# The values of a chunk between the two score rounds of the next one, in a two-layer cross-attention network

## The chip, the cores and the metric

The kernel runs on one core of one Trainium2 chip. The metric is the device time of one execution in microseconds (us); the number quoted is a median over runs. A profile is one further execution, recorded by the hardware profiler, and every duration of a single instruction below comes from it.

## The reference

Two equal layers, each of self-attention, cross-attention to a context, and a gated feed-forward, every one of them after a layer norm and with a residual. All in float32; batch 4, 512 queries, width 320, 20 heads of 16, a context of 1601 rows of width 192.

```
h1 = _ln(x, n1_g, n1_b)
x = _attn(h1, h1, q1, k1, v1, o1_w, o1_b, heads) + x
h2 = _ln(x, n2_g, n2_b)
x = _attn(h2, context, q2, k2, v2, o2_w, o2_b, heads) + x
h3 = _ln(x, n3_g, n3_b)
a, g = jnp.split(h3 @ ff_w1 + ff_b1, 2, axis=-1)
x = a * gelu(g) @ ff_w2 + ff_b2 + x

# _attn, per head
sim = jnp.einsum('bhid,bhjd->bhij', q, k) * scale
out = jnp.einsum('bhij,bhjd->bhid', softmax(sim), v)
```

## The kernel before

**Units and chunks.** Attention is cut into units: one layer, one kind (self or cross), one batch, one group of four heads. Each layer has 20 self units and 20 cross units, so there are 80 in all. The keys of a unit are cut into chunks of 128: four chunks in a self unit (512 keys), thirteen in a cross unit (1601 keys, the last chunk of 65). That makes 160 self chunks and 520 cross chunks, 680 in all. Feed-forward units follow the cross units of each layer.

**A chunk's scores.** For each head of a chunk TensorE (PE) computes a 128x512 tile `st` of scores with keys on the partitions: two products (line 1113, a high and a low part of the queries) and a third matmul that subtracts the row maximum (line 1116). Each uses 32 rows of the array, the rows of its head, so that four such matmuls can run beside each other on four row groups. ScalarE (ACT) then takes the exponential of the tile from PSUM into SBUF (line 1126).

**Two rounds.** A chunk goes in two rounds. The first has the scores of heads 0 and 1, and beside them, on the row groups of heads 2 and 3, two products `sps` (line 926) for the maxima of a coming unit. The second has the scores of heads 2 and 3 and maxima on row groups 0 and 1. VectorE (DVE) reduces the maxima from PSUM (line 947).

**Values.** `values` multiplies the exponentials by the values (line 1141 before, line 1140 after): per chunk four heads, each on 32 columns of the array and 128 rows of keys, all into one PSUM tile `av`. A float32 matmul stands as two matmuls in the trace, so a chunk is eight of them. The result is accumulated in SBUF tile `o`: the first is copied (line 1152), and each later one is copied by ACT to a spare place (line 1157) and added by GpSimd (POOL, line 1158). In the last unit ahead of a feed-forward stage DVE does it instead (line 1154). In cross units `values` takes two chunks at a time, which accumulate in one `av`; in self units one.

**The order on PE.** It is written out by hand, one instruction stream. `main` issues for each chunk the first round, the second round, any extra maxima, then `flush()`, which runs what is in `late`: the values of the chunk (or two chunks) before. Then it appends this chunk's `values` to `late`, and `steps` picks other work off queues (projections of queries, keys and values of coming units, output projections, norms) by due times and credits. Below, this other work on PE is called a step.

**PSUM.** The tiles `st`, `av` and most tiles of the steps come from one pool of four banks, `ps_st`, handed out in turn; so a tile waits until the tile that came four before it has been read. The maxima use a second pool, `ps_m`, of two.

**Places.** Exponentials and the ACT copies of `av` go in turn to thirteen SBUF buffers in cross units and ten in self units (`place`); a buffer is written again when its reader is done.

Of the kernel before, what the change touches and what calls it, by code (L numbers as in the profile page):

```python
# [19 lines left out]
H, DH = 20, 16  # L20
# [3 lines left out]
P = 128  # L24
NQ = N // P
G, HG = 5, 4
GD = HG * DH
SLOT = 32
GT = GD // SLOT

VW = DH + 1
# [33 lines left out]
def kernel(ctx: ExitStack, tc: tile.TileContext, x, context, ws, out):  # L65
# [18 lines left out]
    nc = tc.nc  # L84
# [16 lines left out]
    columns_of = const.tile([P, NC2 * H * VW + SLOT - VW], F32, name="vals")  # L101
# [61 lines left out]
    def place():  # L163
        these = places[at_place["kind"]]
        at_place["i"] = (at_place["i"] + 1) % len(these)
        return these[at_place["i"]]
# [113 lines left out]
    units = []  # L280
# [44 lines left out]
    start = {"on": True, "both": False}  # L325
# [25 lines left out]
    def pick():  # L351
        heads = [
            (q[0][1] + late_by(n), n)
            for n, q in chains.items()
            if q and q[0][2]() and q[0][3]() and (q[0][0][0] != LIGHT or clock["lights"])
        ]
        return min(heads)[1] if heads else None

    def run(chain):
        costs, _, ready, _, f = chains[chain].popleft()  # L360
        assert ready(), chain
        f()
        clock["credit"] -= sum(costs)
# [15 lines left out]
    def next_cost():  # L379
        name = pick()  # L380
        return None if name is None else sum(chains[name][0][0])

    def tick():
        clock["round"] += 1
        clock["credit"] = max(-2.0, min(4.0, clock["credit"] + pace()))

    def steps(beside, lights=1):


        tick()  # L390
        clock["lights"], clock["slots"] = lights, 4
        clock["tiles"] = True if beside is None else None
        done = 0
        while True:
            name = pick()
            if name is None:
                break
            cost = sum(chains[name][0][0])
            if cost >= 0.1:
                share = (2.2, 1.1) if beside else (9.0, 9.0) if beside is False else (0.5, 0.75, 1.5)  # L400
                least = cost * share[done] if done < len(share) else 3.0
                if clock["credit"] < (3.0 if beside is False else least):
                    break
                done += 1
                if clock["tiles"] is not None:
                    clock["tiles"] = name in ALIKE
            run(name)
            if cost == LIGHT:
                clock["lights"] -= 1
            clock["slots"] -= name == "slots"  # L410
        clock["tiles"] = None

    def until(test, name):
        while not test():
            assert chains[name], name
            run(name)
# [570 lines left out]
    def max_reduce(u):  # L987
        if u.pm is not None:
            nc.vector.tensor_reduce(
                u.nm.rearrange("p (j t) -> p t j", t=NQ), u.pm, AX.X, ALU.max, negate=True  # L990
            )
# [89 lines left out]
    late = []  # L1081

    def flush():
        for f in late:
            f()
        late.clear()

    def round_of(scores, maxima):

        todo = [f() for f in scores] + [f() for f in maxima]  # L1090
        for i in range(max((len(passes) for passes, _ in todo), default=0)):
            for passes, _ in todo:
                if i < len(passes):
                    passes[i]()
        for _, then in todo:
            then()

    def main(u, give, nxt):

        pr = {}  # L1100
        if at_place["kind"] != u.kind:
            at_place.update(kind=u.kind, i=min(at_place["i"], len(mine) - 1))

        def score(c, j, st=None):
            r = min(P, u.nkeys - c * P)
            rows = slice(j * SLOT, (j + 1) * SLOT)
            if st is None:
                st = ps_st.tile([P, N], F32, tag="st", name="st")
            keys = u.kT[rows, u.k0 + u.cols[c] : u.k0 + u.cols[c] + r].bitcast(F32R)
            two_rows = slice(j * SLOT, j * SLOT + 2)  # L1110

            def product(e):
                nc.tensor.matmul(st[:r, :], lhsT=keys, rhs=u.q[rows, e, :].bitcast(F32R), start=(e == 0), stop=False)  # L1113

            def less_maximum():
                nc.tensor.matmul(  # L1116
                    st[:r, :],
                    lhsT=units_of[two_rows, :r].bitcast(F32R),
                    rhs=u.mrow[two_rows, :].bitcast(F32R),
                    start=False,  # L1120
                    stop=True,
                )

            def exponential():
                p = place()
                nc.scalar.activation(p[:r], st[:r], AF.Exp)  # L1126
                pr[c, j] = p

            return [lambda: product(0), lambda: product(1), less_maximum], exponential

        last = nxt is None or nxt.kind == "ff"

        def values(cs):
            if u.g in (0, 2):
                until(lambda: units[u.i - u.g].vmade[u.g // 2] > cs[-1], "values")
            ps = ps_st.tile([P, N], F32, tag="st", name="av")
            for c in cs:
                r = min(P, u.nkeys - c * P)
                for j in range(HG):
                    head = (c * H + u.g * HG + j) * VW  # L1140
                    nc.tensor.matmul(  # L1141
                        ps[j * SLOT : (j + 1) * SLOT, :],
                        lhsT=columns_of[:r, head : head + SLOT],
                        rhs=pr.pop((c, j))[:r, :],
                        start=(c == cs[0]),
                        stop=(c == cs[-1]),
                    )
            u.valued = cs[-1] + 1

            if cs[0] == 0:  # L1150
                u.o = three.tile([P, N], F32, tag="o", name="o")
                (nc.vector.tensor_copy if last else nc.scalar.copy)(u.o, ps)
            elif last:
                nc.vector.tensor_tensor(u.o, ps, u.o, ALU.add)
            else:
                vo = place()
                nc.scalar.copy(vo, ps)  # L1157
                nc.gpsimd.tensor_tensor(u.o, u.o, vo, ALU.add)  # L1158
            if u.valued == u.nch:
                add_finish(u)  # L1160


        n = 2 if u.cross else 1
        together = {min(c + n, u.nch) - 1: list(range(c, min(c + n, u.nch))) for c in range(0, u.nch, n)}

        for c in range(u.nch):
            extra = []
            if last:

                both = ps_m.tile([P, 2, N], F32, tag="m", name="st")  # L1170
                round_of([lambda j=j: score(c, j, both[:, j % 2] if j > 1 else None) for j in range(HG)], [])
                tick()
            else:
                for odd in range(2):
                    if odd:
                        tick()
                    pair, rounds = give(2 * c + odd)
                    extra += rounds
                    round_of([lambda j=j: score(c, j) for j in ((2, 3) if odd else (0, 1))], pair)
            u.scored = c + 1  # L1180

            start["both"] = True
            if extra:
                round_of([], extra[0])
            start["both"] = False
            flush()
            if c in together:
                late.append(lambda cs=together[c]: values(cs))
            steps(None, 1 if extra or c == u.nch - 1 else 2)
            for i, e in enumerate(extra[1:]):  # L1190
                if i and next_cost() is not None:
                    run(pick())
                start["both"] = True
                round_of([], e)
                start["both"] = False
            if not last and c == u.nch - 3:
                max_reduce(nxt)
                max_end(nxt)
            if loads:
                loads.popleft()()  # L1200
# [300 lines left out]
```

## Time and profile before

| | |
|---|---|
| runs (us) | 3257.41, 3266.63, 3268.47; median 3266.63 |
| profiled execution (us) | 3267.39; its span, first to last instruction, 3265.6 |
| granted TensorE clock | 0.967 of full speed |
| PE busy | 3117.7 us, 95% of the span |
| DVE busy | 2077.9 us, 64% |
| ACT busy | 1866.6 us, 57% |
| POOL busy | 972.6 us, 30% |
| maxima reduced, line 947 into `pm`, DVE | 980 instructions, mean 1195 ns |
| exponentials, line 1126 into the 8 `pr` buffers, ACT | 1791, mean 602 ns |

Self-attention takes about 30 to 470 us and 1650 to 2050 us of the span, cross-attention about 470 to 1380 us and 2050 to 2990 us, and feed-forward nearly all of the rest. PE counts as busy while any matmul is in its array, and the ends of matmuls are modelled; so a stretch of PE that is "busy" can still hold waits. What a stretch of PE work costs is therefore read from starts: from the first matmul of one kind of work to the first matmul of the next.

### The profile page before, as it was taken

How to read it: one execution, taken by the hardware profiler on the slowest of the kernel's cores; microseconds unless marked ns; L12 is line 12 of the kernel's file. 1: busy time of each engine (PE TensorE's matmuls, PEld its weight loads, DVE VectorE, ACT ScalarE, POOL GpSimd, SP SyncE). 2: the span in 40 equal slices, each digit the busy share in tenths (PEclk: the TensorE clock that was granted, in tenths of full speed). 3: DMA queues.
4: the chain of work that ended last, by engine and by line, in shares of the span. 5: the costliest groups of instructions: out<-in, count | busy, mean ns of one | idle time of the engine just before them, and what ended most of it. 6: DMA issues, size and time to landing. Idle time of an engine off the chain costs nothing.

```text
span 3265.6 us, 89144 instructions
## 1 busy us (share of the span) xinstructions
PE 3117.7 (95%) x36690; PEld 1686.7 (52%) x36690; DVE 2077.9 (64%) x2833; ACT 1866.6 (57%) x3721; POOL 972.6 (30%) x1141
## 2 busy tenths in 40 slices
PE   7899899999999999999998998999999999999999
PEld 3455455555455555455444554555555555554555
DVE  6766777777777776522246777777777777774221
ACT  3666566776667676711126665667767777765110
POOL 2435232323323332111114453324233333322000
PEclk8999899999999999999989998999999999999999
DMA  3433222211212211200113332212112111112000
GB/s 92 91 65 77 44 43 45 54 39 38 65 33 42 60 35 28 80 4 6 27 23 73 72 62 44 41 40 51 33 39 55 36 41 39 39 22 65 9 10 15
DMA packets 213039, 145.08 MB, mean 44 GB/s; under 512 B 65556, under 2 KB 203160, under 8 KB 212632
## 3 DMA queue, kind: packets, MB, share of 16 engines
q1 hardware_dynamic: 211368, 138.32, 19.1%
q8 instruction: 289, 4.73, 0.6%
q10 hardware_dynamic: 1264, 1.06, 0.1%
q14 instruction: 118, 0.97, 0.1%
HBM read 33.04 MB, written 7.93 MB: 13 GB/s over the span
## 4 chain that ended last, share of the span: by engine, by line
PE 80%; DVE 8%; ACT 4%; issue 3%; DMA 2%; SPq 2%; POOL 1%; ACTq 0%; DVEq 0%; POOLq 0%
PE av L1141 19%; PE st L1113 19%; PE fps L1246 9%; PE st L1116 6%; PE yps L1302 5%; PE sps L926 5%; DVE pm L947 3%; PE kps L779 3%; PE qps L717 3%; PE vps L869 3%; PE ops L1050 3%; DVE nmax L947 2%; PE fps L1259 2%; ACT pr L1126 2%; PE kps L749 1%
## 5 line engine op out<-in xcount | busy, mean ns | idle before, releaser
L947 DVE TENSOR_REDUCE pm<-sps 128x2 f32<-128x1024 f32 (+1 forms) x980 | 1127.6, 1195 | 225.3 <-PE sps L926 199.6
L1113 PE MATMUL st<-q,kT 32*128 32x512 f32 (+1 forms) x5440 | 1089.3, 445 | 40.5 <-DVE x L1057 8.0
L1126 ACT ACTIVATE pr<-st 128x512 f32<-128x512 f32 (+1 forms) x1791 | 947.1, 602 | 269.9 <-PE st L1116 252.1
L926 PE MATMUL sps<-kT,q 32*128 32x512 f32 (+1 forms) x6400 | 993.6, 411 | 52.9 <-DMA kT<-stage 20.1
L1113 PEld LDWEIGHTS st<-q,kT 32*128 32x128 f32 (+1 forms) x5440 | 537.6, 182 | 482.3 <-ACT pr L1126 160.2
L1116 PE MATMUL st<-m,units 2*128 2x512 f32 (+1 forms) x2720 | 655.3, 400 | 5.9 <-issue 2.1
L1141 PE MATMUL av<-pr,vals 128*32 128x512 f32 (+1 forms) x3582 | 644.5, 636 | 16.9 <-ACT pr L1126 10.3
L1158 POOL TENSOR_TENSOR o<-o,pr 128x512 f32<-128x512 f32 x236 | 302.2, 1281 | 951.2 <-ACT pr L1157 931.2
L926 PEld LDWEIGHTS sps<-kT,q 32*128 32x128 f32 x6400 | 474.1, 188 | 103.6 <-DVE pm L947 33.3
L947 DVE TENSOR_REDUCE nmax<-sps 128x2 f32<-128x1024 f32 (+1 forms) x356 | 381.2, 1109 | 175.2 <-PE sps L926 121.6
L1126 ACT ACTIVATE wself<-st 128x512 f32<-128x512 f32 (+1 forms) x801 | 427.6, 602 | 75.1 <-PE st L1116 68.6
L1116 PEld LDWEIGHTS st<-m,units 2*128 2x128 f32 (+1 forms) x2720 | 350.7, 184 | 42.8 <-issue 7.7
L1141 PE MATMUL av<-wself,vals 128*32 128x512 f32 (+1 forms) x1602 | 344.5, 635 | 3.6 <-ACT pr L1126 3.0
L1246 PE MATMUL fps<-hT,w 128*128 128x512 f32 x640 | 285.4, 599 | 1.8 <-DVE pr L1272 0.9
L1269 ACT ACTIVATE pr<-fps,b 128x512 f32<-128x512 f32 x80 | 50.6, 683 | 370.4 <-PE fps L1259 268.1
L1141 PEld LDWEIGHTS av<-pr,vals 128*32 128x32 f32 (+1 forms) x3582 | 114.3, 112 | 236.9 <-issue 101.4
L1158 POOL TENSOR_TENSOR o<-o,wself 128x512 f32<-128x512 f32 x89 | 114.0, 1281 | 381.5 <-ACT wself L1157 381.5
L1157 ACT COPY pr<-av 128x512 f32<-128x512 f32 x236 | 140.9, 597 | 135.7 <-PE av L1141 134.7
L1246 PEld LDWEIGHTS fps<-hT,w 128*128 128x128 f32 x640 | 118.9, 190 | 151.8 <-issue 146.6
L624 POOL TENSOR_SCALAR stage<-stage 128x256 fp32r<-128x256 f32 (+1 forms) x155 | 107.1, 691 | 218.6 <-ACT stage L725 135.5
L624 POOL TENSOR_SCALAR w<-w 128x896 fp32r<-128x896 f32 x40 | 98.1, 2452 | 147.0 <-DVE w L789 118.5
L1050 PE MATMUL ops<-wo,aT 112*32 112x160 f32 (+1 forms) x3072 | 128.5, 303 | 4.1 <-ACT pr L1126 2.8
(100 smaller groups left out, 3020.8 us busy)
## 6 DMA issues: line engine op xcount, KB each, us to landing
kT<-w SPq DMA_DIRECT2D x160, 192.0 KB
q<-stage SPq DMA_DIRECT2D x320, 64.0 KB
q<-stage SPq DMA_DIRECT2D x154, 128.0 KB
aT<-o SPq DMA_DIRECT2D x320, 32.0 KB
m<-turned SPq DMA_DIRECT2D x636, 2.0 KB
kT<-stage SPq DMA_DIRECT2D x156, 64.0 KB
w<-in_L_xattn_ff_w_dram SPq DMA_DIRECT2D x20, 256.0 KB
ctxT<-ctxT SPq DMA_DIRECT2D x24, 208.0 KB
```

Of the source, the lines that this page charges most:

```text
L624: eng.tensor_scalar(high.bitcast(F32R), x, 1.0, None, ALU.mult)
L926: nc.tensor.matmul(out, lhsT=u.q[rows, e, queries].bitcast(F32R), rhs=u.kT[rows, keys].bitcast(F32R), start=(e == 0), stop=(e == 1),)
L947: nc.vector.tensor_reduce(to[:, j : j + n], part, AX.X, ALU.max, negate=(ns == 1))
L1050: nc.tensor.matmul(ps[f : f + m, : D // 2], lhsT=aT[:n, k, t * P + f : t * P + f + m], rhs=wo[:n, k, cols], start=(k == 0), stop=(k == 2),)
L1113: nc.tensor.matmul(st[:r, :], lhsT=keys, rhs=u.q[rows, e, :].bitcast(F32R), start=(e == 0), stop=False)
L1116: nc.tensor.matmul(st[:r, :], lhsT=units_of[two_rows, :r].bitcast(F32R), rhs=u.mrow[two_rows, :].bitcast(F32R), start=False, stop=True,)
L1126: nc.scalar.activation(p[:r], st[:r], AF.Exp)
L1141: nc.tensor.matmul(ps[j * SLOT : (j + 1) * SLOT, :], lhsT=columns_of[:r, head : head + SLOT], rhs=pr.pop((c, j))[:r, :], start=(c == cs[0] ...
L1157: nc.scalar.copy(vo, ps)
L1158: nc.gpsimd.tensor_tensor(u.o, u.o, vo, ALU.add)
L1246: nc.tensor.matmul(ps, lhsT=w1[:, k, i * FF + c * P : i * FF + (c + 1) * P], rhs=u.hT[:, k, :], start=ahead and k == 0, stop=not ahead and ...
L1302: nc.tensor.matmul(ps[:, :D], lhsT=hid[c][:, t * P : (t + 1) * P], rhs=w2[:, c, :], start=(c == 0), stop=(c == NHC - 1),)
```

## The change

The body of `values` is the same but for one chunk instead of a list of chunks. In cross units too each chunk now has its own `av` tile and its own evacuation. `flush()` is called once more, between the first and the second round of a chunk, so that the values of the chunk before stand there. The call behind the rounds stays, and finds nothing in `late` except in units whose chunks go in one round (the last unit ahead of a feed-forward stage).

```diff
-        def values(cs):
+        def values(c):
             if u.g in (0, 2):
-                until(lambda: units[u.i - u.g].vmade[u.g // 2] > cs[-1], "values")
+                until(lambda: units[u.i - u.g].vmade[u.g // 2] > c, "values")
             ps = ps_st.tile([P, N], F32, tag="st", name="av")
-            for c in cs:
-                r = min(P, u.nkeys - c * P)
-                for j in range(HG):
...
-                        start=(c == cs[0]),
-                        stop=(c == cs[-1]),
+            r = min(P, u.nkeys - c * P)
+            for j in range(HG):
...
+                    start=True,
+                    stop=True,
...
-        n = 2 if u.cross else 1
-        together = {min(c + n, u.nch) - 1: list(range(c, min(c + n, u.nch))) for c in range(0, u.nch, n)}
-
         for c in range(u.nch):
...
                     round_of([lambda j=j: score(c, j) for j in ((2, 3) if odd else (0, 1))], pair)
+                    if not odd:
+                        flush()
             u.scored = c + 1
...
             flush()
-            if c in together:
-                late.append(lambda cs=together[c]: values(cs))
+            late.append(lambda c=c: values(c))
             steps(None, 1 if extra or c == u.nch - 1 else 2)
```

More of the change, by code (lines that the diff above doesn't have):

```diff
@@ L1131, in main @@
         last = nxt is None or nxt.kind == "ff"
-        def values(cs):
+        def values(c):
             if u.g in (0, 2):
-                until(lambda: units[u.i - u.g].vmade[u.g // 2] > cs[-1], "values")
+                until(lambda: units[u.i - u.g].vmade[u.g // 2] > c, "values")
             ps = ps_st.tile([P, N], F32, tag="st", name="av")
-            for c in cs:
-                r = min(P, u.nkeys - c * P)
-                for j in range(HG):
[L1140 to L1144, printed above, removed]
-                        start=(c == cs[0]),
-                        stop=(c == cs[-1]),
-                    )
-            u.valued = cs[-1] + 1
-            if cs[0] == 0:
+            r = min(P, u.nkeys - c * P)
+            for j in range(HG):
+                head = (c * H + u.g * HG + j) * VW
+                nc.tensor.matmul(
+                    ps[j * SLOT : (j + 1) * SLOT, :],
+                    lhsT=columns_of[:r, head : head + SLOT],
+                    rhs=pr.pop((c, j))[:r, :],
+                    start=True,
+                    stop=True,
+                )
+            u.valued = c + 1
+            if c == 0:
                 u.o = three.tile([P, N], F32, tag="o", name="o")
```

## The prediction

> **What bounds the kernel now.** I read the page first, for the engine that carries the span.
>
> ```profile
> span 3265.6 us, 89144 instructions
> PE 3117.7 (95%) x36690; PEld 1686.7 (52%) x36690; DVE 2077.9 (64%) x2833; ACT 1866.6 (57%) x3721; POOL 972.6 (30%) x1141
> PE 80%; DVE 8%; ACT 4%; issue 3%; DMA 2%; SPq 2%; POOL 1%; ACTq 0%; DVEq 0%; POOLq 0%
> ```
>
> PE is the bound (95% busy, 80% of the chain that ended last); the rest has room. But PE executes in order, and a "busy" PE can still be waiting with a matmul in flight. So I then read the timeline of single chunks, PE and ACT side by side (columns: start, length, engine, line, what). First a cross chunk that stands between two calls of values:
>
> ```profile
> 645.24 0.50 PE L1113 MATMUL st<-q,kT 32*128 32x512 f32 x2
> 645.58 0.40 PE L1113 MATMUL st<-q,kT 32*128 32x512 f32 x2
> 645.81 0.40 PE L1116 MATMUL st<-m,units 2*128 2x512 f32 x1
> 646.07 0.49 PE L1113 MATMUL st<-q,kT 32*128 32x512 f32 x1
> 646.31 1.09 ACT L1126 ACTIVATE pr<-st 128x512 f32<-128x512 f32 x2 [0.29 <-PE st L1116]
> 646.42 0.61 PE L1116 MATMUL st<-m,units 2*128 2x512 f32 x2
> 646.96 1.07 PE L1141 MATMUL av<-pr,vals 65*32 65x512 f32 x8
> 647.96 0.45 PE L779 MATMUL kps<-ctxT,w 32*64 32x224 f32 x8
> ```
>
> Three things are to be seen. Matmuls of 512 columns follow each other by phases: 0.34 us after the first, then 0.23. Two adjacent rounds share a phase, because the second round's heads are on the row groups that the first has left: five phases for a chunk, not six. And the values start at 646.96, which is 0.05 us after the first exponential is over (646.31 + 0.60 = 646.91): their `av` tile takes the bank of `st` of head 0. So a chunk costs 1.72 us from its first score to the values, where five phases with the passage at the end would be 0.33 + 3 x 0.23 + 0.33 = 1.35.
>
> Second, two chunks in a row with nothing between, and the values of two chunks behind:
>
> ```profile
> 908.43 0.50 PE L1113 MATMUL st<-q,kT 32*128 32x512 f32 x2
> 910.14 0.98 PE L1113 MATMUL st<-q,kT 32*128 32x512 f32 x2 [0.26 <-ACT pr L1126]
> 911.20 0.91 PE L1113 MATMUL st<-q,kT 32*128 32x512 f32 x2
> 911.98 0.60 PE L1116 MATMUL st<-m,units 2*128 2x512 f32 x2
> 912.51 0.63 PE L1141 MATMUL av<-wself,vals 128*32 128x512 f32 x3
> ```
>
> From 908.43 to 912.51: 4.08 us for two chunks, where ten phases need 2.50. The second chunk waits for exponentials to give banks back. Third, a block of only three phases, from a chunk without maxima:
>
> ```profile
> 1351.43 0.74 PE L1113 MATMUL st<-q,kT 32*128 32x512 f32 x8
> 1351.99 0.41 PE L1116 MATMUL st<-m,units 2*128 2x512 f32 x4
> 1352.33 1.06 PE L1141 MATMUL av<-pr,vals 65*32 65x512 f32 x8
> ```
>
> It takes 0.90 us. Last, two rows of the costliest groups, for what a call of values leaves to other engines:
>
> ```profile
> L1158 POOL TENSOR_TENSOR o<-o,pr 128x512 f32<-128x512 f32 x236 | 302.2, 1281 | 951.2 <-ACT pr L1157 931.2
> L1157 ACT COPY pr<-av 128x512 f32<-128x512 f32 x236 | 140.9, 597 | 135.7 <-PE av L1141 134.7
> ```
>
> **Off PE.** The cross units now evacuate 13 times instead of 7: 38 units x 6 = 228 more copies of 0.59 us on ACT (135 us, 57% to about 59%) and 228 more adds of 1.28 us on POOL (292 us, 30% to about 37%). In the two last units 12 adds of 0.69 us go to DVE (8 us). I price all this at nothing: POOL stays idle for over half of the time, and an exponential that takes over a place that POOL reads comes thirteen places later, now 2.6 chunks (some 8 us) instead of 2.9. If that cover failed, each late add would hold an exponential, and the values and PE behind it, for up to 1.28 us.
>
> **On PE, block by block.** The order of PE's instructions in both programs gives the blocks, that is stretches of one kind of work. Without extra maxima and without the last units, before has 345 score blocks of one chunk, 97 of two; values of two chunks stand 129 times before scores and 109 times before a step, values of one 57 and 141 times. Medians from first matmul to the next block's first matmul, over the whole trace: 1.71, 4.07; 1.854, 1.741, 0.996, 0.882. The sum is 590 + 395 + 239 + 190 + 57 + 124 = 1595 us. 101 blocks with extra maxima (85 of one chunk, 16 of two) hold 145 + 66 = 211 us of the same; the extra maxima themselves stay.
>
> After, the scores fall apart: 655 blocks of a single round, 266 of two rounds (the second of a chunk and the first of the next, where no step stands between them), 74 and 21 with extra maxima, and 674 calls of values, all with scores behind them. Score blocks go from 565 to 1053 in all.
>
> One round alone: three phases, 0.33 + 0.23 + 0.33 = 0.90. No such block is in the trace with two heads and two maxima. The nearest row is the block of 1351.43, the same three phases, so I take 0.90. It can't be less; it can be no more than the 1.71 of two rounds. Two of them cost 1.80 where the chunk cost 1.71: the phase that adjacent rounds shared is lost and a passage is added, but the wait for the bank (0.37) goes, since `av` now takes a bank whose exponential ran long before.
>
> A two-round block: here a new wait comes. The values behind it are those of the chunk whose second round has only just opened the block. Subtracting the maximum starts 0.57 after the block does, ends 0.40 later, ACT starts 0.10 later, two exponentials take 1.09, and PE starts 0.05 after them: 0.57 + 0.40 + 0.10 + 1.09 + 0.05 = 2.20 us, against 1.35 that PE needs. ACT is free for it: the copy of the `av` before begins about 0.2 into the block and is over by 0.8, the exponentials can start at 1.07. Queued behind the waiting values on PE are the chunk's next second round and any step; ACT waits for that round in turn. The bounds are 1.35 (nothing waits) and 2.79 (the copy gets between, 0.59).
>
> Where a step does stand between the rounds, the shortest (query projections, about 0.8 us) gives 0.90 + 0.8 + 0.90 = 2.6, more than 2.20, so there the values find their exponentials done.
>
> The sum after: 655 x 0.90 + 266 x 2.20 + 674 x 0.996 = 590 + 585 + 671 = 1846; with extra maxima 74 x 0.90 + 21 x 2.20 = 113; the last units 24 x 1.8 = 43, before 12 x 1.9 = 23. Context values on row tiles, like the scores, lose a passage each: 64 x 0.25 = 16 off. So after 1846 + 113 + 43 - 16 = 1986, before 1595 + 211 + 23 = 1829: 157 us more. From this I take 25 us, because in the self stages PE is idle for 84 us (840 us, 756 busy) for other engines, and some of the added time lies in those waits. That leaves +132 us on 3267.4: 3399, call it 3400. The profiled execution is 0.8 us above the median of the runs, so no correction is made.
>
> **A rule that speaks against the change.** In the trace a passage from scores to values starts 0.325 us after the last phase where nothing waits, against a pitch of 0.23, and from values to scores 0.523 against 0.43: 0.19 us for leaving and returning, 488 times more often, 92 us; this is already inside the block times. The Trainium skill, TensorEngine Tiling (Array Packing), section Key Properties, says that a change of tiling mode drains TensorE, but gives no price. The Trainium skill, TensorE: Matmul & The Clock Gate, section Step-by-step: what each phase is for, has about 128 cycles for a drain; an estimate from that page, at its 2.4 GHz, is 53 ns each, 52 us for 976 passages, and the forecast would be some 40 us lower by it; I keep the trace's rows.
>
> **Rivals.** (1) Faster: the values don't wait for the last exponential in a two-round block. Then it costs 1.35, 266 x 0.85 = 226 us less, and the kernel comes to 3400 - 226 = 3174; the place is the `av` matmul behind the second round, and with 2.20 - 132/266 = 1.70 us per block the change would be even. For it: the two-chunk blocks lose 1.57 us each to banks now, and the change breaks these up. Against it: the five terms of 2.20 are each read from rows above and follow one another. (2) Slower by more: one-round blocks wait too, because ACT, with its 228 more copies and the steps' evacuations in its order, is behind at short steps, or POOL holds a place. Half the 1.09 us of two exponentials on half of the blocks is 655 x 0.27 = 180 us: 3580. For it: the exponentials are on the chain at every chunk now. Against: 2.6 us of cover against 2.20. (3) No change: PE's stalls now (block means exceed the medians, and PE is idle for 148 us in all) absorb all that is added: 3267. Against: 520 of the 680 chunks are cross chunks, and in the cross stages (2030 us) PE is idle for only 48 us. That the change does nothing is no rival, since the order of instructions differs.
>
> **How the numbers follow.** A measurement of this kernel can tell about 0.3% (10 us) from no change. The forecast has 0.82; its own range is 3320 to 3470, from a two-round block of 1.90 (80 us less) to one-round blocks of 1.00 (65 us more). Rival 1 and partial forms of it 0.06, rival 2 0.09, rival 3 0.03. The range is 3320 to 3480, with a little of rival 2. Chances: faster 0.06, same 0.03, slower 0.91.
>
> **What would show it.** Right: in the profile after, `av` waits for ACT `pr` or `wself` (line 1126) for many times the 22 us that it has now; blocks of two rounds take 2.2 us and of one round 0.9; adds on POOL go from 348 to 576; PE's share falls to about 92%. Wrong: two-round blocks near 1.4, one-round blocks over 1.1, exponentials that wait for POOL, or maxima that wait for banks.

## The result, and the profile after

The changed kernel takes 3388.81 us (median of 4 runs, 3378.96 to 3391.92), the kernel before 3267.55 (4 runs): ratio 1.0365, 95% interval 1.0324 to 1.0406. It is slower by 121 us; the forecast was 132 us, 3400. The page of the changed kernel, its span, its engines and the shares of the chain that ended last:

```profile
span 3388.5 us, 89789 instructions
PE 3274.0 (97%) x36690; PEld 1625.3 (48%) x36690; DVE 2123.4 (63%) x2846; ACT 2027.4 (60%) x3949; POOL 1264.9 (37%) x1369
PE 84%; DVE 9%; SPq 3%; DMA 2%; issue 1%; ACT 1%; POOL 1%; ACTq 0%; DVEq 0%; POOLq 0%
```

PE has the same 36690 matmuls and is "busy" for 156 us more. Where that is can be read in a timeline of PE and ACT (start, length, engine, line): a two-round block, which begins with the second round of one chunk and ends with the first round of the next, the values behind it, and a one-round block.

```profile
742.57 0.50 PE L1113 MATMUL st<-q,kT 32*128 32x512 f32 x2
742.76 0.59 ACT L1156 COPY wself<-av 128x512 f32<-128x512 f32 x1
743.13 0.40 PE L1116 MATMUL st<-m,units 2*128 2x512 f32 x1
743.62 2.06 ACT L1126 ACTIVATE wself<-st 128x512 f32<-128x512 f32 x4 [0.28 <-PE st L1116]
744.28 0.62 PE L1140 MATMUL av<-pr,vals 128*32 128x512 f32 x2
744.75 1.06 PE L1140 MATMUL av<-wself,vals 128*32 128x512 f32 x3
745.74 0.50 PE L1113 MATMUL st<-q,kT 32*128 32x512 f32 x2
746.30 0.41 PE L1116 MATMUL st<-m,units 2*128 2x512 f32 x2
746.64 0.86 PE L717 MATMUL qps<-hT,w 112*32 112x128 f32 x24
```

ACT starts the exponentials at 743.62; the second is over at 744.71 (0.60 + 0.49 later), and the values of the last head start within the row of 744.75. The values' first three heads began at 744.28, 0.06 us after the first exponential (743.62 + 0.60) had given its bank back. So block and values take 745.74 - 742.57 = 3.17 us; the prediction had 2.20 + 1.00. Over the trace the median of this sum is 3.175 us, in 254 blocks that carry eight maxima matmuls. The one-round block goes from 745.74 to 746.64: 0.90 us, the median 0.90 as well.

Two signs in the profile that the prediction got wrong. PE's share rose to 97% and did not fall to 92%, and the waits of PE say next to nothing of the values:

```profile
PE sps L926 <- DVE pm L947: 26.9, 26, 1.5
PE av L1140 <- ACT pr L1126: 0.8, 3, 0.3
```

The reason is in the timeline: the values' last head waits while the other three are in the array, so PE counts as busy. The wait shows in the length of the values (1.457 us median behind such a block, 0.996 elsewhere), not in an idle time. Nor did the waits of the values' weight loads for exponentials grow: for those in `pr` and `wself` together 177 us before (133.3 and 44.1), 176 after (113.9 and 62.4).

Off PE, the groups of the evacuation are as forecast; the adds on POOL are 576 over all places (348 before), and ACT's exponentials wait less than 1 us for them:

```profile
L1157 POOL TENSOR_TENSOR o<-o,pr 128x512 f32<-128x512 f32 x377 | 483.0, 1281 | 804.7 <-ACT pr L1156 799.0
L1156 ACT COPY pr<-av 128x512 f32<-128x512 f32 x377 | 221.3, 587 | 45.8 <-PE av L1140 42.1
```

### The profile page after: what moved, and what is told of

The parts are those of the page before. It is cut to its first block, busy times and chain, and to the rows that moved or that the text cites. A ratio compares the mean times of both kernels' runs of the same rounds, so it can differ in the third digit from the quotient of the medians.

```text
span 3388.5 us, 89789 instructions
## 1 busy us (share of the span) xinstructions
PE 3274.0 (97%) x36690; PEld 1625.3 (48%) x36690; DVE 2123.4 (63%) x2846; ACT 2027.4 (60%) x3949; POOL 1264.9 (37%) x1369
## 3 DMA queue, kind: packets, MB, share of 16 engines
q14 instruction: 124, 1.02, 0.1%
## 4 chain that ended last, share of the span: by engine, by line
PE 84%; DVE 9%; SPq 3%; DMA 2%; issue 1%; ACT 1%; POOL 1%; ACTq 0%; DVEq 0%; POOLq 0%
PE av L1140 21%; PE st L1113 20%; PE fps L1242 8%; PE st L1116 7%; PE yps L1298 5%; PE sps L926 4%; PE qps L717 3%; DVE pm L947 3%; PE kps L779 3%; PE ops L1050 3%; PE vps L869 2%; PE fps L1255 2%; DVE nmax L947 2%; PE vps L851 2%; PE kps L749 2%; SPq L1006 2%
## 5 line engine op out<-in xcount | busy, mean ns | idle before, releaser
L947 DVE TENSOR_REDUCE pm<-sps 128x2 f32<-128x1024 f32 (+1 forms) x980 | 1150.8, 1196 | 369.4 <-PE sps L926 354.2
L1113 PE MATMUL st<-q,kT 32*128 32x512 f32 (+1 forms) x5440 | 1059.3, 455 | 15.1 <-DVE pm L947 5.4
L926 PE MATMUL sps<-kT,q 32*128 32x512 f32 (+1 forms) x6400 | 1016.1, 419 | 45.5 <-DVE pm L947 26.9
L1113 PEld LDWEIGHTS st<-q,kT 32*128 32x128 f32 (+1 forms) x5440 | 468.0, 186 | 783.0 <-issue 340.8
L1157 POOL TENSOR_TENSOR o<-o,pr 128x512 f32<-128x512 f32 x377 | 483.0, 1281 | 804.7 <-ACT pr L1156 799.0
L1140 PE MATMUL av<-pr,vals 128*32 128x512 f32 (+1 forms) x3582 | 761.3, 628 | 7.6 <-DVE nmax L947 2.6
L1116 PE MATMUL st<-m,units 2*128 2x512 f32 (+1 forms) x2720 | 611.4, 407 | 21.5 <-DMA m<-turned 18.7
L1140 PE MATMUL av<-wself,vals 128*32 128x512 f32 (+1 forms) x1604 | 418.0, 621 | 1.4 <-DVE pm L947 0.7
L1157 POOL TENSOR_TENSOR o<-o,wself 128x512 f32<-128x512 f32 x175 | 224.6, 1284 | 315.6 <-ACT wself L1156 314.8
L1116 PEld LDWEIGHTS st<-m,units 2*128 2x128 f32 (+1 forms) x2720 | 304.2, 187 | 79.1 <-issue 28.3
L1156 ACT COPY pr<-av 128x512 f32<-128x512 f32 x377 | 221.3, 587 | 45.8 <-PE av L1140 42.1
```

The source lines that it names most:

```text
L926: nc.tensor.matmul(out, lhsT=u.q[rows, e, queries].bitcast(F32R), rhs=u.kT[rows, keys].bitcast(F32R), start=(e == 0), stop=(e == 1),)
L947: nc.vector.tensor_reduce(to[:, j : j + n], part, AX.X, ALU.max, negate=(ns == 1))
L1116: nc.tensor.matmul(st[:r, :], lhsT=units_of[two_rows, :r].bitcast(F32R), rhs=u.mrow[two_rows, :].bitcast(F32R), start=False, stop=True,)
L1140: nc.tensor.matmul(ps[j * SLOT : (j + 1) * SLOT, :], lhsT=columns_of[:r, head : head + SLOT], rhs=pr.pop((c, j))[:r, :], start=True, stop= ...
```

## The experiments

The change has two halves: the values go one chunk at a time, and they stand between the rounds. The first four kernels take these apart, and the wait from the rest.

**Single chunks behind both rounds.** The changed kernel without the call in the middle:

```diff
-                    if not odd:
-                        flush()
```

> One half of the change alone: values one chunk at a time, but still behind both score rounds. Theory A (the cost of the change is the wait of the values for the exponentials of the round that stands just ahead, plus a small loss per split chunk): nothing is split here, and the 97 two-chunk score blocks with two chunks of values behind (4.07 + 1.85 us) become two chunks at 1.71 + 1.00 each, so 97 x 0.5 = 48 us less, some 4 us more for passages: about 3224 us, faster than before. Rival B (the cost is passages between kinds of PE work: 121 us for 488 more score blocks, 0.25 us each): 689 score blocks instead of 565, 124 x 0.25 = 31 us more: about 3298 us.

Measured: 3226.97 us, ratio to before 0.9873 (0.985 to 0.9895), granted clock 0.968. The forecast of theory A (3224) holds, that of rival B (3298) does not: there are 124 more score blocks than before and the kernel is 41 us faster. So passages (changes on PE from one kind of work to another) alone do not set the time, and of the two halves this one is a gain; the place between the rounds costs 3389 - 3227 = 162 us. This kernel beats both others. What bounds its chunk is the wait that the prediction read in the profile of before, now at most chunks. PE and ACT in its timeline, and the waits of weight loads (PEld), which show a wait that PE's own rows hide:

```profile
902.79 0.60 ACT L1126 ACTIVATE pr<-st 128x512 f32<-128x512 f32 x1 [0.65 <-PE st L1116]
903.44 1.07 PE L1140 MATMUL av<-pr,vals 128*32 128x512 f32 x8 [0.27 <-ACT pr L1126]
PEld av L1140 <- ACT pr L1126: 197.9, 410, 0.9
```

The values start 0.05 us after the end of the first exponential of the two rounds just ahead (902.79 + 0.60 = 903.39): their `av` tile takes the bank of that score tile.

**Pairs between the rounds.** The kernel before with the call in the middle:

```diff
+                    if not odd:
+                        flush()
```

> The other half alone: values between the two rounds, but two chunks of a cross unit at a time as before. Theory A, by block prices (score blocks of one round 0.90, of three about 2.9, of four 4.07; values of two chunks 1.85): the first chunk of a pair covers most of the wait for the second chunk's exponentials, and the two-chunk stalls of before stay: about 55 us more than before, 3320 us. Rival B: 815 score blocks, 250 x 0.25 = 62 us more, 3329 us. This run does not tell A from B; it tells the place from the cutting into single chunks.

Measured: 3415.95 us, 1.0467 (1.0436 to 1.0498): the slowest of all, 96 us over the expectation. The blocks of four rounds, 45 of them, take 5.12 us on average where I had 4.07 (the 31 that no window of half clock touches 4.78), those of three rounds about 3.15 where I had 2.9, and the granted clock of its runs has the median 0.952. What makes the four rounds longer at full clock was not taken apart. The changed kernel, with single chunks at the same place, is 27 us faster.

**Values one chunk later.** The changed kernel with

```diff
-    def flush():
-        for f in late:
-            f()
-        late.clear()
+    def flush(keep=0):
+        while len(late) > keep:
+            late.pop(0)()
...
-                        flush()
+                        flush(1 if u.cross and c else 0)
...
-            flush()
+            flush(1 if u.cross and not last else 0)
```

> The changed kernel, with the values of a cross unit run one chunk later still (between the rounds of chunk c stand the values of chunk c-2, not c-1; at the first chunk of a unit both that are left). PE's blocks are nearly the same (1015 score blocks, 1053 in the changed kernel). Theory A: the values find their exponentials done; a two-round block with its values goes from 3.18 us to what ACT needs per chunk (four exponentials 2.06, one copy 0.59, gaps 0.1: 2.75 us) or less, so about 205 x 0.43 = 88 us less than the changed kernel: 3300 us, down to 3230 if PE's own 2.35 us were reached. Rival B: no change but for 38 blocks, about 3380 us.

Measured: 3387.19 us, 1.036 (1.0312 to 1.0409), no change against the changed kernel. At the block it did what theory A said: two-round block and values fell from 3.175 to 2.725 us (median of 178). But the time didn't follow. The granted clock of its four runs has the median 0.9475, against 0.9615, some 46 us at 3.3 us per 0.001 (see the end); and since the second chunk of a unit has no values between its rounds now, 37 blocks of three or four rounds came back, at 3.1 to 4.7 us each. In its profile the values take 89 us less than in the changed kernel, scores with maxima 57 us more and the steps 8 us more.

**Cross units only.** The call in the middle stands in cross units alone:

```diff
-                    if not odd:
+                    if not odd and u.cross:
                         flush()
```

> The changed kernel with the new place in cross units only; self units have their values behind both rounds as before. Theory A: in self units the change cost 0.2 us per chunk with a step behind it (98) and 0.5 per chunk without (57), 48 us, part of it in waits that are there anyway: about 35 us less than the changed kernel, 3354 us. Rival B: 922 score blocks, 131 x 0.25 = 33 us less. If self chunks hide the cost wholly, 3389 us.

Measured: 3368.28 us, 1.0311 (1.0288 to 1.0334). The self units bear 21 us of the 162; theory A's prices give 48 there. That the rest lies in waits that the self stages have anyway is argued, not shown. Theory A (3354) and rival B (3356) both missed, and this run does not tell them apart.

**A constant in place of the exponentials.** To take away the wait of the values for exponentials, in the changed kernel and, as a control, in that with single chunks behind. The values no longer read the exponentials, so what these kernels compute is not the attention; and no exponential waits any more for a place to be read:

```diff
+            steady = units_of.rearrange("p (o w) -> p o w", o=1).to_broadcast([P, 4, P])
...
-                    rhs=pr.pop((c, j))[:r, :],
+                    rhs=steady[:r],
```

> The changed kernel, with a constant tile in place of the exponentials as the moving operand of the values (the exponentials are computed and not read). PE's order, the evacuations and the banks are the same; only the wait of the values for the exponentials is gone, and what is left is the wait for the bank of the score tile of head 2. Theory A: a two-round block with its values goes from 3.18 us to 1.72 + 1.00 = 2.72 us, about 270 x 0.46 = 124 us less, 3265 us; each 0.001 of granted clock that it gains or loses moves that by 3 us (four runs of the kernel with values one chunk later: 0.952 at 3366.7 us, 0.942 at 3401.6 us). Rival B (passages between kinds of PE work): no change, 3389 us. Rival C (the granted clock alone, which falls where score rounds and values alternate): 3380 us or more, at the same clock of about 0.96.

> The control: the kernel with single chunks of values behind both rounds, with the same constant tile as the moving operand of the values. There the exponentials that the values read are a whole chunk old, and the values wait only for the bank of head 0, which stays. Theory A and B: no change, 3227 us within 10. If reading a constant itself changes time or clock, it shows here.

Measured: 3342.53 us, 1.0224 (1.0187 to 1.0261), clock 0.9545 (median of its runs), and the control 3225.26, 0.9866 (0.983 to 0.9902). The control stands still, as it should. The changed kernel gains 46 us: rivals B and C (no change) fall, but 124 us were expected. The median of block and values went from 3.175 to 2.727, just as expected. Two things took from it. More blocks are long for another reason (at full clock 23% of the two-round blocks take over 1.9 us, 17% in the changed kernel): mostly maxima that wait for a bank from DVE, or scores that wait for a transfer of the row maxima; the waits of PE in this kernel:

```profile
PE sps L926 <- DVE pm L947: 33.6, 33, 1.8
PE st L1116 <- DMA m<-turned: 23.2, 18, 2.2
```

(26.9 and 18.7 us in the changed kernel). At full clock the mean of block and values so falls by 0.316 us (3.262 to 2.946, 225 and 221 blocks), where the medians fall by 0.448; on 225 blocks that is 71 us, on all 254 it would be 80. And the granted clock fell by 0.007, worth about 23 us (3.3 us per 0.001, see the end). 71 - 23 = 48, near the 46 that were measured, but only as an estimate. The whole profile shows the same trade: values 104 us less than in the changed kernel, scores with maxima 39 us more, steps 15 us more.

**Exponentials of half the columns.** Both kernels with the constant, and half of each exponential left out:

```diff
-                nc.scalar.activation(p[:r], st[:r], AF.Exp)
+                nc.scalar.activation(p[:r, : N // 2], st[:r, : N // 2], AF.Exp)
```

> The changed kernel with the constant operand in the values and exponentials of half the columns (128x256, 0.38 us by the ACT rows of that shape, not 0.60). ACT then needs about 1.9 us per chunk. Theory A': what kept the constant operand from giving its whole 124 us was ACT, which in runs of chunks without steps is behind and holds banks; then a two-round block with its values goes from a mean of 3.18 us to 2.50 (bank of head 2: 0.57 + 0.40 + 0.10 + 0.38 + 0.05, and values 1.00) plus 0.15 for half-clock windows, 254 x 0.5 = 130 us less than with whole exponentials: about 3210 us. Theory D: it was the granted clock; then the blocks at full clock gain and more windows at half clock take it back, 3280 us or more. On the clock itself: if it falls because PE waits, it comes back to 0.967 here; if it falls because rounds, values and steps alternate one by one, it stays at about 0.955.

> The control, single chunks of values behind both rounds, constant operand, exponentials of half the columns. The values wait for the bank of head 0, so for one exponential: a chunk goes from 1.72 to 1.50 us in about 600 blocks, 0.22 x 600 = 130 us less: about 3095 us, granted clock 0.967 or above. If the wait ahead of the values were not the bank of head 0, the time would stay at 3225 us.

Measured: 3319.86 us, 1.0164 (1.0129 to 1.02), clock 0.956, and the control 3181.56, 0.9759 (0.9721 to 0.9797), clock 0.968. Theory A' (3210) and the control's 3095 both missed. In the control the wait for the first exponential is confirmed where a step comes ahead (1.71 to 1.51 us, medians of 269 blocks), but where values come ahead the block falls only from 1.84 to 1.725 (229 blocks). In the changed kernel the two-round block stays at 1.73 us. Theory A' is refuted: shorter exponentials do not shorten this block. The time fits the bound of theory D (3280 or more), but not its reason, since blocks at full clock did not gain (with values 2.94 and 2.96 us on average). The timeline of the changed kernel so altered, PE and ACT:

```profile
743.60 0.50 PE L1113 MATMUL st<-q,kT 32*128 32x512 f32 x2
743.79 0.59 ACT L1157 COPY wself<-av 128x512 f32<-128x512 f32 x1 [0.37 <-PE av L1141]
744.18 0.75 PE L1113 MATMUL st<-q,kT 32*128 32x512 f32 x2
744.44 0.49 PE L926 MATMUL sps<-kT,q 32*128 32x512 f32 x2
745.33 1.07 PE L1141 MATMUL av<-units,vals 128*32 128x512 f32 x8
```

The copy of `av` ends at 744.38, and 0.06 us later the second head of the next chunk and its maxima start: that score tile takes the bank of `av`. Over the trace this fourth score tile of a two-round block starts 0.053 us after the end of the copy (median; between 0.03 and 0.09 us in 227 of 232 blocks at full clock), 0.83 us into the block; in the control, behind a step, where no copy is in the way, 0.59 us into it. So 0.19 + 0.59 + 0.06 = 0.84, and three phases with the passage, 0.89, make 1.73. In the changed kernel the same chain is there (0.053 us after the copy in 231 of 236 blocks), beside that of the first exponential, and ends at the same time; take one away and the other stands. No run takes away the copy, so what a block without it would cost is not shown. On the clock, this kernel kept 0.956 with the shorter exponentials and the control 0.968: here the clock went with the order on PE.

## Why the prediction was right

**The total.** 121 us measured, 132 forecast. Block by block: one round 0.90 (forecast 0.90), two rounds with values 3.175 (3.196), values elsewhere 0.996 (0.996), POOL and ACT hidden (forecast so; single chunks behind the rounds have the same evacuations and are faster than before). The two halves have opposite signs, which the prediction's sum held but did not say: single chunks -41 us, the place +162. The place comes apart like this: the wait for exponentials 71 us (the constant operand); split chunks, 364 one-round blocks ahead of a step, where a chunk with its values costs 0.90 + 0.996 + 0.90 = 2.80 against 1.71 + 0.88 = 2.59, 0.21 each or 76 us; and the clock, 0.9675 to 0.9615, about 20 us. Sum 167, measured 162. Only the first of the three was taken away by itself; the second is worked out from medians, the third from the spread of runs. The profiles give a check that needs no prices, from starts over the whole span, single chunks behind the rounds against the changed kernel: values 142 us more, scores with maxima 19, steps 3, together 164.

That the total came within 11 us is in part luck. By the same starts, scores, maxima and values take 113 us more than before, where the sum had 157 ahead of the 25 that were taken off: it counted medians, and the values of before took 674 us where their medians give 610. The steps take 10 us more, and the granted clock fell from 0.966 to 0.9615 (medians), some 15 us; the prediction had nothing for either.

**What failed.** The step "the bounds are 1.35 (nothing waits)", on which rival 1 stood: without the wait the block is 1.73, not 1.35, and the copy of `av` fits that: it holds a bank that the next scores need. I had the copy end 0.8 into the block and looked only at ACT, where it was in nobody's way; the bank behind it was the cost. The wait stood in the prediction's first timeline already. The row of ACT between those shown there is

```profile
645.43 0.58 ACT L1157 COPY pr<-av 128x512 f32<-128x512 f32 x1 [0.86 <-PE av L1141]
```

and the single score matmul at 646.07 starts 0.06 us after its end (646.01). So where values come directly ahead of a block, its 1.72 us are not the exponential's wait alone. Rival 1 and its 3174 us, with 1.35 us per block, could thus not be had from the exponentials alone. At 1.73 us the block is near the even point of 1.70, and still the changed kernel with no wait of the values for exponentials is 2.2% slower than before: the even point took the other blocks and the clock as fixed, and neither stayed. The signs to look for in the profile after were wrong too, as shown above: a partial wait inside a group of matmuls is busy time. The term of 25 us for the self stages was close to what the cross-only kernel leaves of theory A's price there, 48 - 21 = 27, but that 48 is itself a forecast.

## What to carry to other kernels

Before work is put between two pieces that ran beside each other in the array, price the phase they shared, the passage, and the age of its operands in the new place: here the values came to stand 1.35 us of PE work behind the scores whose exponentials need 2.20. When a wait is to go, write down every chain that ends at that point, buffers that are handed on included, because the second one is often as long; a half of the change alone, run by itself, can be the better kernel (0.9873 of before). And read PE by distances between starts, since a busy share of 97% here was slower than one of 95%.

## What the runs showed of the hardware

In these runs the granted clock went with the order on PE. It comes as full or half in the record, in windows of 3.4 us and multiples (one shorter window in each trace): before, 46 windows and 216 us at half; the changed kernel 34 and 265 us; values one chunk later 41 and 323 us. Two spans with their mean clocks, single chunks behind the rounds and values one chunk later:

```profile
core 0: 3224.8 us, clock 0.968
core 0: 3364.9 us, clock 0.952
```

The three test kernels with values behind the rounds have medians of 0.9675, 0.9665 and 0.968, the kernel before beside them 0.966, 0.965 and 0.968; all with values between them in every unit lie between 0.9475 and 0.9615, and with cross units alone at 0.9615. The same program also varies from run to run: values one chunk later took 3366.7 us at 0.952 and 3401.6 at 0.942, 3.5 us per 0.001, and the kernel before 3260.97 at 0.969 and 3276.28 at 0.964, 3.1 us. I use 3.3. The windows give the same: 265 us at half clock in a span of 3388.5 make a mean of 0.961, so 0.001 is 6.8 us at half clock, 3.4 us of full-speed work. What in the alternation takes the clock away was not settled; shorter exponentials did not bring it back.

The Trainium skill, TensorE: Matmul & The Clock Gate, section A second HAM failure mode: psum-queue depth-cycling, describes a kernel whose matmul groups cycle through PSUM banks with short idle times between them, and whose clock swings between half and full. The swing is what the windows here show; that short idle times cause it is not shown by any run here.
